# Attention values in four column tiles, and key tiles added in pairs, in a pre-norm transformer block (f32)

## The chip, the cores and the metric

The kernel runs on one core of a Trainium2 chip. The metric is the device time of one execution in microseconds (us), as the median of several runs. A core has five engines that run side by side, each with its own queue in order: TensorE (PE, products; PEld is its loading of stationary operands), VectorE (DVE), ScalarE (ACT), GpSimd (POOL) and SyncE (SP, which issues DMAs). They wait for one another through semaphores.

## The reference

A transformer block on x of shape 2 x 1024 x 1024 in float32: attention of 32 heads of width 32, then a gated feed-forward layer, both behind a layer norm and with a residual.

```python
qkv = x @ attn_qkvw + attn_qkvb                      # x: layer-normed
scores = einsum('bhqd,bhkd->bhqk', q, k) * scale     # 32 heads, 1024 queries, 1024 keys
probs = softmax(scores, axis=-1)
ctx = einsum('bhqk,bhkd->bhqd', probs, v)
x = x + ctx @ attn_ow + attn_ob
...
y = silu(xn @ W_gate.T) * (xn @ W_up.T) @ W_down.T   # 2752 wide; xn: layer-normed x
x = x + y
```

## The kernel before

The program is one long list of steps in Python, which emits instructions; what it emits first stands first in each engine's queue. `Emitter.run` (L66) merges two lists: a *fill* list of projections and feed-forward products, and a *paced* list, the attention. Each step has a planned cost (`MM4` = 855 ns for a 512-column f32 product). Attention steps that are marked as a beat are spread evenly over the planned cost of the fill; the paced steps that follow a beat are emitted at once behind it. A third kind, `em.later(delay, ...)`, is emitted when the planned clock has passed the delay.

`attention_steps` (L581) lays out the 64 heads (2 batches of 32) in beats n, eight key tiles of 128 keys to a head. One beat holds:

- `scores(kt)` (L490): two products of 512 queries into a PSUM tile `s` of 128 keys x 1024 queries; ACT copies it to `p` (L502); DVE takes the running maximum over the head's key tiles into `top` (L505, L507). With the last key tile comes `maximum()` (L511): two transposes and two reductions on DVE (L517, L518), and later a product, a reduction and two DMAs that spread the negative maximum to the tile `m`.
- `less_maximum` (L542) of the key tile 10 beats back: p + m, on DVE for key tiles 3 and 7, on POOL for the other six.
- `exponential` (L547) of the key tile 11 beats back, on ACT.
- `values` (L550) of the key tiles 12 beats back, four at a time: in the beat where key tile 3 or 7 is due, those of tiles 0 to 3 or 4 to 7 are emitted one after another.

The stationary operand of `values` is a tile `vones` of 64 columns for each key tile: the head's 32 values columns (loaded by `load_v`, L483, from DRAM on SP's queue, two beats before the head's last scores) and 32 columns of ones, written once. So one product gives 32 rows of values and 32 rows of sums. The 1024 queries are taken as two halves of 512, which go to two column tiles of TensorE (output partitions 0 to 63 and 64 to 127) and accumulate over the eight key tiles in one PSUM tile `acc`. Each f32 product leaves two records of loading and two of multiplying in the trace. `finish` (L565) copies `acc` to SBUF on ACT and stores the values and one row of the sums to DRAM, four DMA issues per head on SP's queue. There, the sums' reciprocals are made later and multiplied on by `prep_ctx` (L626).

The attention steps are cut in two lists at beat 272, that is 34 heads. The first list is paced over the projections of both batches, the second over the rest of the projections and the output projection and feed-forward layer of batch 0. During the first, POOL also builds sums of the weights (`weight_sum_steps`, L1067) for the feed-forward products (L853, L994). Batch 1's feed-forward layer runs last, without attention.

Of the kernel before, what the change touches and what calls it, by code (L numbers as in the profile page):

```python
# [24 lines left out]
class Steps:  # L25
# [6 lines left out]
    def add(self, fn, cost=0.0, needs=None, gives=None, beat=False):  # L32
        self.items.append((fn, cost, needs, gives, beat))
# [97 lines left out]
def preln_block_kernel(  # L131
# [26 lines left out]
    HPG = P // HD  # L158
    SCALE = 1.0 / math.sqrt(HD)
    MM4, MM1 = 855.0, 230.0  # L160
    QTR = 4
    LAG = 2
    RUN = 4
    RING = NT + LAG + RUN + 2

    const = ctx.enter_context(tc.tile_pool(name="const", bufs=1))
# [23 lines left out]
    def Sm(name, dt=F32):  # L190
        return ltile([P, NH], *(("S", 6) if dt == F32 else ("Sr", 3)), name, dt)
# [17 lines left out]
    def dtile(shape, name):  # L209
        return dram.tile(shape, F32, tag=name, name=name)  # L210
# [19 lines left out]
    em = Emitter()  # L230
# [212 lines left out]

    vones = [const.tile([P, NT, 2, HD], F32, tag=f"vones{i}", name=f"vones{i}") for i in range(2)]
    for t in vones:
        nc.gpsimd.memset(t[:, :, 1, :], 1.0)


    part = const.tile([P, P], F32, tag="part", name="part")
    nc.vector.memset(part, 0.0)

    class Head:
# [3 lines left out]
        def __init__(self, b, h):  # L458
            self.b, self.h, self.g = b, h, h // HPG
            self.hf = self.g // (G // NHF)  # L460
            self.name = f"{b}_{h}"
            self.v = vones[(b * HEADS + h) % 2]
            self.p = {}

        def load(self, i):

# [16 lines left out]
        def load_v(self):  # L483
            c = (self.h * HD) % NH
            nc.sync.dma_start(
                self.v[:, :, 0, :],
                dv[self.b, self.hf][:, c : c + HD].rearrange("(c p) n -> p c n", p=P),
            )

# [57 lines left out]
        def exponential(self, kt):  # L547
            nc.scalar.activation(self.p[kt], self.p[kt], AF.Exp, scale=SCALE)  # L548

        def values(self, kt):  # L550

            if kt == 0:
                self.acc = psum.tile([P, NH], F32, tag="acc", bufs=1, name=f"acc_{self.name}")
            for s in range(NS):
                nc.tensor.matmul(  # L555
                    self.acc[s * 2 * HD : (s + 1) * 2 * HD, :],
                    self.v[:, kt, :, :].rearrange("p a n -> p (a n)"),
                    self.p[kt][:, s * NH : (s + 1) * NH],
                    start=(kt == 0),
                    stop=(kt == NT - 1),  # L560
                )
            if kt == NT - 1:
                self.finish()

        def finish(self):  # L565
            part, n = divmod(self.h, HEADS // QTR)
            cs = Sm(f"cs_{self.name}")
            nc.scalar.copy(cs, self.acc)

            def store(s):  # L570
                r = 2 * s * HD
                cols = slice(s * NH, (s + 1) * NH)
                nc.sync.dma_start(
                    dctx[self.b, part][n * HD : (n + 1) * HD, cols], cs[r : r + HD, :]
                )
                nc.sync.dma_start(dsum[self.b, part][n : n + 1, cols], cs[r + HD : r + HD + 1, :])

            em.later(2500.0, lambda: store(0))
            em.later(2600.0, lambda: store(1), ("ctx", self.b, self.h))

    def attention_steps(cut):  # L581


        heads = [Head(b, h) for b in range(B) for h in range(HEADS)]
        lists = [Steps(), Steps()]
        total = len(heads) * NT
        q = lists[0]

        def load_step(k, i):
            if k < len(heads):  # L590
                q.add(lambda: heads[k].load(i), needs=("qk", heads[k].b, heads[k].g))

        for i in range(3):
            load_step(0, i)
        for n in range(total + NT + LAG + 2):
            if n == cut:
                q = lists[1]
            k, kt = divmod(n, NT)
            if n < total:
                if kt % 2 == 0 and kt < 6:  # L600
                    load_step(k + 1, kt // 2)
                if n == 0:
                    q.add(lambda: em.later(9000.0, lambda: None, ("first",)))
                    q.add(lambda: None, needs=("first",))
                if kt == NT - 2:
                    q.add(heads[k].load_v, needs=("v", heads[k].b, heads[k].hf))
                q.add(lambda k=k, kt=kt: heads[k].scores(kt), 2 * MM1, beat=True)
            else:
                q.add(lambda: None, beat=True)
            k, kt = divmod(n - NT - LAG, NT)  # L610
            if 0 <= k < len(heads):
                needs = ("max", heads[k].b, heads[k].h)
# [13 lines left out]
    def prep_ctx(b):  # L626


        def recip(i):
            cols = HEADS // QTR * S // P  # L630
            sm = small([P, cols], "sums", 1, f"sums_{b}_{i}")
            flat = lambda d: d.rearrange("h s -> (h s)").rearrange("(p c) -> p c", p=P)
            nc.sync.dma_start(sm, flat(dsum[b, i]))
            rc = small([P, cols], "recs", 1, f"recs_{b}_{i}")

            def go():
                nc.vector.reciprocal(rc, sm)
                nc.sync.dma_start(flat(drec[b, i]), rc)

            em.later(7000.0, go, ("rec", b, i))  # L640
# [487 lines left out]
    with tc.manual_schedule():  # L1128
# [80 lines left out]
            keep.items.insert(0, ffn0.items.pop())  # L1209
        tail(ffn1, 1)  # L1210

        first, second = attention_steps(HEADS * NT + 16)
# [58 lines left out]
```

## Time and profile before

| what | value |
|---|---|
| median of 3 runs | 3316.62 us (3312.51 to 3321.08) |
| the profiled execution | 3320.87 us, its span 3319.1 us |
| mean granted TensorE clock | 0.995 |
| L494, scores products | 1024 records, 467.0 us busy |
| L366, projection products | 1024 records, 469.6 us busy |
| L853, feed-forward products of 256 columns | 4704 records in two groups, 610.5 and 464.7 us busy |
| L548 on ACT, exponentials | 512 of 1060 ns |
| L502 on ACT, copies of scores | 512 of 1010 ns |
| L507 on DVE, maxima | 384 of 1222 ns |
| DMA, share of 16 engines | 41.1% and 12.2% on its two large queues |

The span runs from the first to the last instruction of the profiled execution; the rest of that execution's time lies around it. Busy time of an engine is the time in which at least one of its instructions ran: on TensorE several can run at once, so that a group's busy time is less than its count times its mean. Idle time is that of the engine just before the instruction, with the instruction or DMA that ended it.

### The profile page before, as it was taken

How to read it: one execution, taken by the hardware profiler on the slowest of the kernel's cores; microseconds unless marked ns; L12 is line 12 of the kernel's file. 1: busy time of each engine (PE TensorE's matmuls, PEld its weight loads, DVE VectorE, ACT ScalarE, POOL GpSimd, SP SyncE). 2: the span in 40 equal slices, each digit the busy share in tenths (PEclk: the TensorE clock that was granted, in tenths of full speed). 3: DMA queues.
4: the chain of work that ended last, by engine and by line, in shares of the span. 5: the costliest groups of instructions: out<-in, count | busy, mean ns of one | idle time of the engine just before them, and what ended most of it. 6: DMA issues, size and time to landing. Idle time of an engine off the chain costs nothing.

```text
span 3319.1 us, 34091 instructions
## 1 busy us (share of the span) xinstructions
PE 3246.9 (98%) x11456; PEld 1883.5 (57%) x11456; DVE 1767.1 (53%) x2454; ACT 1358.8 (41%) x1520; POOL 1187.0 (36%) x584
## 2 busy tenths in 40 slices
PE   8999998999999999999999999999999999999999
PEld 4444343444444446666664566666557777476775
DVE  3455555555555466666656675566434333344434
ACT  2465565656666455555563555555200000010000
POOL 0377666666775543333335333333210000200000
PEclk9999998999999999999999999999999999999999
DMA  4665665566555635555555455554545555645553
GB/s 166 198 210 175 204 219 183 161 211 203 191 191 168 200 108 151 154 157 153 152 164 181 127 153 158 155 154 138 166 159 153 153 153 149 196 143 152 154 153 96
DMA packets 336702, 548.64 MB, mean 165 GB/s; under 512 B 104976, under 2 KB 104976, under 8 KB 336528
## 3 DMA queue, kind: packets, MB, share of 16 engines
q1 hardware_dynamic: 281360, 414.31, 41.1%
q10 hardware_dynamic: 55168, 132.15, 12.2%
q8 instruction: 92, 1.51, 0.2%
q14 instruction: 82, 0.67, 0.1%
HBM read 454.30 MB, written 92.01 MB: 165 GB/s over the span
## 4 chain that ended last, share of the span: by engine, by line
PE 81%; DMA 6%; DVE 3%; POOL 3%; ACT 3%; issue 2%; ACTq 0%; SPq 0%; POOLq 0%; DVEq 0%
PE p L853 30%; PE pd L994 14%; PE acc L555 10%; PE pq L366 7%; PE po L711 6%; PE s L494 5%; PE pvv L422 5%; DMA m<-d 2%; POOL p L545 2%; PE pd L926 2%; DMA d<-neg 2%; ACT p L502 1%; POOL ws L1105 1%; DVE top L507 1%; PE pg L897 1%
## 5 line engine op out<-in xcount | busy, mean ns | idle before, releaser
L545 POOL TENSOR_TENSOR p<-p,m 128x1024 f32<-128x1024 f32 x384 | 928.4, 2444 | 995.3 <-DMA m<-d 717.7
L502 ACT COPY p<-s 128x1024 f32<-128x1024 f32 x512 | 516.9, 1010 | 630.7 <-PE s L494 595.9
L507 DVE TENSOR_TENSOR top<-s,top 128x1024 f32<-128x1024 f32 x384 | 469.1, 1222 | 551.1 <-ACT p L502 548.5
L548 ACT ACTIVATE p<-p 128x1024 f32<-128x1024 f32 x512 | 542.1, 1060 | 251.4 <-POOL p L545 236.8
L853 PE MATMUL p<-sum,m 128*128 128x256 f32 x2688 | 610.5, 381 | 2.7 <-DVE sum L764 1.9
L853 PEld LDWEIGHTS p<-sum,m 128*128 128x128 f32 x2688 | 508.6, 190 | 92.0 <-issue 15.2
L494 PE MATMUL s<-qs,ks 128*128 128x512 f32 x1024 | 467.0, 537 | 22.8 <-DVE top L507 22.8
L366 PE MATMUL pq<-xnT,wqk 128*128 128x512 f32 x1024 | 469.6, 596 | 0.0
L555 PE MATMUL acc<-p,vones 128*64 128x512 f32 x2048 | 468.2, 599 | 0.5 <-ACT p L548 0.4
L853 PE MATMUL p<-xn2T,m 128*128 128x256 f32 x2016 | 464.7, 380 | 0.7 <-DVE gate L876 0.7
L994 PE MATMUL pd<-wp,h 128*128 128x512 f32 x960 | 429.3, 594 | 0.2
L853 PEld LDWEIGHTS p<-xn2T,m 128*128 128x128 f32 x2016 | 380.0, 190 | 73.9 <-issue 17.0
L494 PEld LDWEIGHTS s<-qs,ks 128*128 128x128 f32 x1024 | 186.5, 191 | 233.8 <-issue 147.1
L994 PEld LDWEIGHTS pd<-wp,h 128*128 128x128 f32 x960 | 180.1, 190 | 214.3 <-issue 192.4
L366 PEld LDWEIGHTS pq<-xnT,wqk 128*128 128x128 f32 x1024 | 194.4, 191 | 187.4 <-issue 175.0
L555 PEld LDWEIGHTS acc<-p,vones 128*64 128x64 f32 x2048 | 135.3, 136 | 267.7 <-issue 211.4
L1007 DVE TENSOR_TENSOR x<-pd,x 128x512 f32<-128x512 f32 x360 | 236.8, 684 | 83.3 <-PE pd L994 83.3
L916 POOL MEMSET h<- 64x512 f32 x4 | 2.1, 524 | 678.1 <-PE pd L994 678.1
L881 ACT ACTIVATE gate<-gate 128x512 f32<-128x512 f32 x84 | 52.9, 630 | 464.5 <-DVE gate L880 464.3
L422 PE MATMUL pvv<-wv,xnT 128*128 128x512 f32 x512 | 236.8, 600 | 1.5 <-ACT xnT L267 0.9
L711 PE MATMUL po<-wo,ctx 128*128 128x512 f32 x512 | 227.6, 594 | 0.0
L545 DVE TENSOR_TENSOR p<-p,m 128x1024 f32<-128x1024 f32 x128 | 182.5, 1426 | 0.0
(90 smaller groups left out, 2049.4 us busy)
## 6 DMA issues: line engine op xcount, KB each, us to landing
m<-dws SPq DMA_DIRECT2D x336, 256.0 KB
m<-in_w_gu SPq DMA_DIRECT2D x252, 256.0 KB
wp<-ddn SPq DMA_DIRECT2D x160, 256.0 KB
qs<-dq ACTq DMA_DIRECT2D x64, 512.0 KB
ks<-dq ACTq DMA_DIRECT2D x128, 256.0 KB
m<-d SPq DMA_DIRECT2D x64, 512.0 KB
wp<-in_w_dn SPq DMA_DIRECT2D x120, 256.0 KB
raw<-in_w_gu ACTq DMA_DIRECT2D x84, 256.0 KB
```

The costliest lines, as they stand in the source:

```text
L366: nc.tensor.matmul(ps, wqk[b, g, w, hk][:, k, :], xnT[b, s][:, kc, :], start=(kc == 0), stop=(kc == KC - 1),)
L422: nc.tensor.matmul(st["ps"], xnT[b, t // TB][:, kc, (t % TB) * P : (t % TB + 1) * P], st["w"][kc], start=(kc == 0), stop=(kc == KC - 1),)
L494: nc.tensor.matmul(ps[:, s * NH : (s + 1) * NH], k[:, kt * P : (kt + 1) * P], q[:, s * NH : (s + 1) * NH], start=True, stop=True,)
L502: nc.scalar.copy(p, ps)
L507: nc.vector.tensor_tensor(self.top, ps, self.top, ALU.max)
L545: eng.tensor_tensor(p, p, self.m, ALU.add)
L548: nc.scalar.activation(self.p[kt], self.p[kt], AF.Exp, scale=SCALE)
L555: nc.tensor.matmul(self.acc[s * 2 * HD : (s + 1) * 2 * HD, :], self.v[:, kt, :, :].rearrange("p a n -> p (a n)"), self.p[kt][:, s * NH : ( ...
L711: nc.tensor.matmul(st["ps"], ctxT[b, blk][:, g, t * P : (t + 1) * P], st["w"][hf, g], start=(g == 0), stop=(g == G - 1),)
L853: nc.tensor.matmul(ps, mats[c, n][:, kc, :], rhs, start=(kc == 0), stop=(kc == hk - 1),)
L994: nc.tensor.matmul(st["pd"], lefts[n](pi)[:, j, t * P : (t + 1) * P], st["wp", pi, n, j], start=(j == 0), stop=(j == PART // 2 - 1),)
L1007: nc.vector.tensor_tensor(xs, st["pd"], xs, op)
```

## The change

Each key tile's values are computed with a stationary operand of 32 columns, the values alone (`vals`), by four products of 256 queries, one to each column tile of TensorE (output partitions 32j to 32j + 31), into the first 256 columns of `acc`. The sums come from four more products with a stationary tile of ones, into the last 256 columns.

Some key tiles are added in pairs: for a tile kt in `added`, its exponentials become p[kt] + p[kt-1]. The values of tile kt - 1 are replaced by v[kt-1] - v[kt] (`differences`, on POOL, once per head, for all its pairs), so that p[kt-1] (v[kt-1] - v[kt]) + (p[kt] + p[kt-1]) v[kt] is the same sum of values, and the ones products of tile kt - 1 are left out, since the added tile holds its exponentials. For heads 0 to 33 `added` is (1, 5), and both additions are on DVE. For heads 34 to 63 it is (1, 3, 5, 7): tiles 1 and 5 are added on POOL, tiles 3 and 7 on DVE.

The addition is emitted one beat after the tile's exponential, ahead of the values if those are due in the same beat. The planned cost of a tile's values is `MM4`, or half of it where the ones are left out. A head's results are stored by two DMA issues in place of four.

```diff
+    CUT = HEADS * NT + 16
...
-    vones = [const.tile([P, NT, 2, HD], F32, tag=f"vones{i}", name=f"vones{i}") for i in range(2)]
-    for t in vones:
-        nc.gpsimd.memset(t[:, :, 1, :], 1.0)
+    vals = [const.tile([P, NT, HD], F32, tag=f"vals{i}", name=f"vals{i}") for i in range(2)]
+    ones = const.tile([P, HD], F32, tag="ones", name="ones")
+    nc.gpsimd.memset(ones, 1.0)
+    NQ = S // HPG
...
+            self.added = (1, 5) if (b * HEADS + h) * NT < CUT else (1, 3, 5, 7)
...
+        def differences(self):
+            step = self.added[1] - self.added[0]
+            v = self.v.rearrange("p (i a) n -> p i a n", a=step)[:, :, :2, :]
+            nc.gpsimd.tensor_tensor(v[:, :, 0, :], v[:, :, 0, :], v[:, :, 1, :], ALU.subtract)
+
+        def add(self, kt):
+            if kt in self.added:
+                late = kt % RUN == RUN - 1 or len(self.added) == NT // RUN
+                eng = nc.vector if late else nc.gpsimd
+                eng.tensor_tensor(self.p[kt], self.p[kt], self.p[kt - 1], ALU.add)
+
         def values(self, kt):
             if kt == 0:
                 self.acc = psum.tile([P, NH], F32, tag="acc", bufs=1, name=f"acc_{self.name}")
-            for s in range(NS):
-                nc.tensor.matmul(
-                    self.acc[s * 2 * HD : (s + 1) * 2 * HD, :],
-                    self.v[:, kt, :, :].rearrange("p a n -> p (a n)"),
-                    self.p[kt][:, s * NH : (s + 1) * NH],
-                    start=(kt == 0),
-                    stop=(kt == NT - 1),
-                )
+            def columns(w, c, start, stop):
+                for j in range(HPG):
+                    nc.tensor.matmul(
+                        self.acc[j * HD : (j + 1) * HD, c : c + NQ],
+                        w,
+                        self.p[kt][:, j * NQ : (j + 1) * NQ],
+                        start=start,
+                        stop=stop,
+                        skip_group_check=True,
+                    )
+
+            columns(self.v[:, kt, :], 0, kt == 0, kt == NT - 1)
+            if kt + 1 not in self.added:
+                columns(ones, NQ, False, kt == NT - 1)
...
-            em.later(2500.0, lambda: store(0))
-            em.later(2600.0, lambda: store(1), ("ctx", self.b, self.h))
+            em.later(2500.0, store, ("ctx", self.b, self.h))
...
+                if kt == 0:
+                    q.add(heads[k].differences)
                 needs = ("max", heads[k].b, heads[k].h)
                 q.add(lambda k=k, kt=kt: heads[k].less_maximum(kt), needs=needs)
...
-            if 0 <= k < len(heads) and kt % RUN == RUN - 1:
-                for v in range(kt - RUN + 1, kt + 1):
-                    q.add(lambda k=k, v=v: heads[k].values(v), MM4)
+            if 0 <= k < len(heads):
+                q.add(lambda k=k, kt=kt: heads[k].add(kt))
+                if kt % RUN == RUN - 1:
+                    for v in range(kt - RUN + 1, kt + 1):
+                        cost = MM4 / 2 if v + 1 in heads[k].added else MM4
+                        q.add(lambda k=k, v=v: heads[k].values(v), cost)
```

More of the change, by code (lines that the diff above doesn't have):

```diff
@@ L461, in __init__ @@
             self.name = f"{b}_{h}"
-            self.v = vones[(b * HEADS + h) % 2]
+            self.v = vals[(b * HEADS + h) % 2]
             self.p = {}
+            self.added = (1, 5) if (b * HEADS + h) * NT < CUT else (1, 3, 5, 7)
         def load(self, i):
@@ L485, in load_v @@
             nc.sync.dma_start(
-                self.v[:, :, 0, :],
+                self.v,
                 dv[self.b, self.hf][:, c : c + HD].rearrange("(c p) n -> p c n", p=P),
@@ L568, in finish, with store @@
             nc.scalar.copy(cs, self.acc)
-            def store(s):
-                r = 2 * s * HD
-                cols = slice(s * NH, (s + 1) * NH)
+            def store():
+                ctx_ = dctx[self.b, part][n * HD : (n + 1) * HD, :]
                 nc.sync.dma_start(
-                    dctx[self.b, part][n * HD : (n + 1) * HD, cols], cs[r : r + HD, :]
-                )
-                nc.sync.dma_start(dsum[self.b, part][n : n + 1, cols], cs[r + HD : r + HD + 1, :])
-            em.later(2500.0, lambda: store(0))
-            em.later(2600.0, lambda: store(1), ("ctx", self.b, self.h))
+                    ctx_.rearrange("f (j q) -> j f q", j=HPG),
+                    cs[:, :NQ],
+                )
+                sums = dsum[self.b, part][n, :].rearrange("(j q) -> j q", j=HPG)
+                nc.sync.dma_start(sums, cs[::HD, NQ:])
+            em.later(2500.0, store, ("ctx", self.b, self.h))
     def attention_steps(cut):
@@ L1210, in preln_block_kernel @@
         tail(ffn1, 1)
-        first, second = attention_steps(HEADS * NT + 16)
+        first, second = attention_steps(CUT)
         prep0, prep1 = prep_ctx(0), prep_ctx(1)
```

## The prediction

> **What bounds the kernel now.** I read the page first (shares, chain, costliest groups), then the busy time of three stretches, then the timeline around one head's values products, then TensorE's idle gaps and the clock after them. Columns of a group: line, engine, operation, out<-in and shapes, count | busy us, mean ns of one | idle us before and who ended it.
>
> ```profile
> PE 3246.9 (98%) x11456; PEld 1883.5 (57%) x11456; DVE 1767.1 (53%) x2454; ACT 1358.8 (41%) x1520; POOL 1187.0 (36%) x584
> PE 81%; DMA 6%; DVE 3%; POOL 3%; ACT 3%; issue 2%; ACTq 0%; SPq 0%; POOLq 0%; DVEq 0%
> L545 POOL TENSOR_TENSOR p<-p,m 128x1024 f32<-128x1024 f32 x384 | 928.4, 2444 | 995.3 <-DMA m<-d 717.7
> L555 PE MATMUL acc<-p,vones 128*64 128x512 f32 x2048 | 468.2, 599 | 0.5 <-ACT p L548 0.4
> L545 DVE TENSOR_TENSOR p<-p,m 128x1024 f32<-128x1024 f32 x128 | 182.5, 1426 | 0.0
> ```
>
> TensorE is busy 98% of the span and is 81% of the chain; the products that the change touches wait 0.5 us in all. So TensorE sets the time: a product saved is time saved, and a new wait in its queue is time lost in full.
>
> ```profile
> 1144.00:1770.00 626.00, 617.72 (x2375) 382.68 (x2375) 397.27 (x543) 338.64 (x362) 243.66 (x109) 1.00 0.52 156
> 139.00:1144.00 1005.00, 960.02 (x3013) 421.35 (x3011) 555.63 (x595) 601.29 (x655) 667.37 (x333) 0.99 0.60 192
> ```
>
> Stretches (length, then busy PE, PEld, DVE, ACT, POOL, clock, DMA share, GB/s). Heads 0 to 33 run in 139 to 1144 us, heads 34 to 63 until 2379 us. In the second stretch TensorE idles 8 us of 626, so nothing there can absorb a wait.
>
> The timeline where head 41's first four key tiles are multiplied (start, us, engine, line):
>
> ```profile
> 1435.72 1.03 PE L494 MATMUL s<-qs,ks 128*128 128x512 f32 x2
> 1436.67 3.65 PE L555 MATMUL acc<-p,vones 128*64 128x512 f32 x16
> 1436.84 1.01 ACT L502 COPY p<-s 128x1024 f32<-128x1024 f32 x1 [3.65 <-PE s L494]
> 1437.88 1.23 DVE L507 TENSOR_TENSOR top<-s,top 128x1024 f32<-128x1024 f32 x1 [0.20 <-ACT p L502]
> 1439.21 0.71 DVE L517 STREAM_TRANSPOSE m<-top 128x512 f32<-128x512 f32 x1
> 1439.96 0.69 DVE L518 TENSOR_REDUCE part<-m 128x16 f32<-128x512 f32 x1
> 1440.56 0.70 DVE L517 STREAM_TRANSPOSE m<-top 128x512 f32<-128x512 f32 x1
> 1441.30 0.69 DVE L518 TENSOR_REDUCE part<-m 128x16 f32<-128x512 f32 x1
> ```
>
> A scores product (L494) is followed at once by the values products (L555): 16 records in 3.65 us, two abreast, a pair every 0.43 us (the weight loads of such a group start at 1438.01, 1438.44, 1438.87). While TensorE multiplies, the same scores go through ACT's copy, DVE's maximum and, for a head's last key tile, four more DVE instructions, until 1441.99, 5.3 us after the group began.
>
> **Part 1, products saved.** Two records of 512 columns take 0.43 us side by side. Now a key tile's values are 8 records of 256 columns in four tiles: four abreast they also take 0.43 us, and its ones another 0.43. Before, a head took 16 x 0.43 = 6.88 us. A tile whose successor is added needs no ones: heads 0 to 33 have 8 + 6 = 14 groups of 8 (6.02 us), the rest 8 + 4 = 12 (5.16 us). Saved: 34 x 0.86 + 30 x 1.72 = 29 + 52 = 81 us. The trace shows two abreast, never four. Bounds per group: 0.43 (four) and 0.86 (the two abreast of L555). I take 0.43: the pair's records start 7 ns apart and each runs as fast as a lone one, and neither waits for the other's second pass, so tiles look independent.
>
> The Trainium skill speaks against it: TensorE: Matmul & The Clock Gate, section Back-to-back issue gap, gives about 81 ns for each load-and-multiply pair in a stream of 128-column products. No run here has so dense a stream. By that page's figure a group of 8 would take an estimated 0.65 us and the whole change would come to about 3,695 us.
>
> **Part 2, the new wait (heads 34 to 63).** Key tiles 3 and 7 are added on DVE, and the add stands in DVE's queue directly behind the maximum of the scores product that precedes the values group on TensorE (for tile 3, behind the four head-maximum instructions too). Values of tile 3 wait for the add. In the rows above: maxima done at 1441.99, add 1.43 us (L545 on DVE, same shapes), landing 0.05 later: 1443.47. TensorE gets through tiles 0 to 2 (1 + 2 + 1 groups, 1.72 us) at 1438.39. Stall 5.1 us. Read so for each head from 34 to 62, the stall is 5.1 us in the median and 152 us in all; for tile 7, where only copy and maximum stand before the add, 2.2 us in the median and 77 us over 28 heads. (Head 62's second half and head 63 have no scores ahead of them: no stall.) Behind the waiting product stand the next scores and all of the feed-forward products; they go late by the full stall, since the stretch has no idle time to give back. Sum 229 us; bounds 57 less each 1.72 (131, if groups take 0.86) and 229.
>
> Heads 0 to 33 add tiles 1 and 5, two beats ahead of the values: their exponential ends 4.9 us (median) before the group, so an add of 1.43 fits. Cover gone, each would cost up to 1.43.
>
> **Part 3, the clock after a stall.** TensorE's idle gaps of this trace (in brackets) and the clock behind them:
>
> ```profile
> 544.75 1.11 PE L259 MATMUL pt_a<-ident,x 128*128 128x128 f32 x4 [5.21 <-DVE lo L381]
> 1771.58 2.93 PE L926 MATMUL pd<-wd,h 128*128 128x512 f32 x3 [4.44 <-DVE x L1007]
> 575.17 0.73 PE L494 MATMUL s<-qs,ks 128*128 128x512 f32 x2 [1.86 <-DVE top L507]
> ...
> 541.90:548.80 6.90, 4.05 (x9) 2.57 (x10) 5.31 (x6) 6.06 (x8) 6.90 (x5) 0.51 0.45 142
> 576.10:579.50 3.40, 3.40 (x5) 1.33 (x4) 3.37 (x5) 1.96 (x2) 3.40 (x3) 0.50 0.07 13
> 1770.70:1777.60 6.90, 6.02 (x7) 2.53 (x8) 6.90 (x7) 1.06 (x1) 5.19 (x2) 0.51 0.00 0
> ```
>
> All three gaps over 4.4 us led to 6.8 us at half clock, with 4.0 to 6.0 us of products in it: 2.7 us lost each on average. Of six gaps from 1.8 to 2.6 us three led to 3.4 us at half clock, 1.7 lost. So 29 x 2.7 + 28 x 0.85 = 102 us. Bounds: 0 (the 3.5 us gap at 386 us had no drop) and 29 x 3.0 + 28 x 1.7 = 135.
>
> The same page of the Trainium skill, Part 1, lets the clock fall after an idle window of about 3.4 us; by that the 2.2 us stalls are free and the long ones cost an estimated 1.7 us, 49 in all. The 1.86 us gap above contradicts it, so the rows count.
>
> **Part 4, the rest.** DVE gets 34 x 2 x 1.43 = 97 us in the first stretch, where it is 55% busy; 97 is the bound if none is hidden, 0 if all. TensorE now waits there some 73 us for L507; with 97/556 more DVE work I take 17% of that, 13 us. POOL gets 30 x 2 adds of 2.44 us (row L545 on POOL) and 64 small differences; POOL is 39% busy in the second stretch and idles 26 us per head waiting for m, and v has landed at least 11 us before the first L545 of each head, so 0; uncovered, 2.44 each, 146 us. The exponentials before POOL's adds of tiles 1 and 5 end 13 us (median) ahead of the values, so these are not waited for: 0. Stores go from four DMA issues per head to two on SP: 0. The planner counts the products at the new, lower cost; its delays only grow in real time: 0.
>
> **Sum.** 3320.9 (profiled execution) - 81 + 13 + 229 + 102 = 3584; the median of the runs lies 4 us under that execution: **3580 us**.
>
> **Rivals.** (a) The clock stays up: 3580 - 102 = 3478. For: one 3.5 us gap without a drop; against: three of three longer ones. (b) Fewer than four abreast. At 0.86 per group: 34 x 5.16 + 30 x 3.44 = +278 in place of -81, stalls 131, clock about 25 (gaps of 3.4 us), 13: 3321 + 447 - 4 = 3764. For: four abreast is nowhere in the trace, and 16 instructions per 0.43 us is four times what L555 needs now. Against: the independent pairs. (c) Faster: the add is done when TensorE comes to tile 3 (7), because DVE takes it before the maximum. Then 3317 - 81 + 13 = 3249. It decides as soon as the stalls and their clock cost less than 68 us in all, some 1.2 us each. Against: the queue order above, and copy plus maximum plus add alone are 3.7 us against 1.72. (d) The change does not take place: the built program has 4,640 more matmul records and 128 more DVE instructions; no weight.
>
> **How the numbers follow.** Forecast 0.55, its own range 3530 to 3620 (clock 50 to 135); (a) or a partial drop 0.16; (b) and between 0.24; (c) 0.04, and 0.01 for a result within 0.3%, which is what measurement can tell from no change. The range leaves out the lowest of (a), (c) and the end of (b): 3465 to 3730. Faster 0.04, same 0.01, slower 0.95.
>
> **What would show it.** Right: L575 groups with TensorE idle some 5 and 2 us before tile 3 and 7, released by the DVE add, from 1144 us on only; half clock in that stretch; heads 0 to 33 in slightly less time than 1005 us. Wrong: no idle time at L575 from DVE, or the first stretch growing (then four abreast fails).

## The result, and the profile after

The changed kernel takes 3742.43 us (median of 4 runs, 3726.51 to 3747.26), the kernel before 3317.97 us: a ratio of 1.127 [1.124, 1.131]. The profiled execution has a span of 3742.5 us at a mean granted clock (the share of its full speed that TensorE was granted) of 0.947; before, 3319.1 us at 0.995.

From the page of the changed kernel: busy time by engine, the clock in 40 slices, the shares of the chain, and three of the costliest groups (columns as in the prediction):

```profile
PE 3332.1 (89%) x16096; PEld 2007.1 (54%) x16096; DVE 2028.9 (54%) x2582; ACT 1360.5 (36%) x1520; POOL 1417.8 (38%) x707
PEclk9999999999999999888888989989999999999999
PE 48%; DVE 10%; ACT 2%; issue 2%; DMA 1%; POOL 0%; SPq 0%; ACTq 0%; DVEq 0%; POOLq 0%
L498 PE MATMUL s<-qs,ks 128*128 128x512 f32 x1024 | 476.8, 547 | 46.1 <-DVE top L511 46.1
L575 PE MATMUL acc<-p,vals 128*32 128x256 f32 x4096 | 327.4, 412 | 289.4 <-DVE p L565 289.4
L575 PE MATMUL acc<-p,ones 128*32 128x256 f32 x2592 | 229.1, 429 | 0.0
```

The values products, which waited 0.5 us in the kernel before, now wait 289 us for the addition (L565) on DVE; the scores products (L498) wait 46 us for DVE's maximum. The clock digits show the loss where heads 34 and on run.

Windows of the changed kernel, cut at head 0's first values group, head 34's, and the last one's end (length, busy PE, PEld, DVE, ACT, POOL, clock, DMA share, GB/s):

```profile
138.90:1226.40 1087.50, 967.26 (x5736) 474.12 (x5735) 670.05 (x664) 600.83 (x655) 712.11 (x368) 0.96 0.57 177
1226.40:2797.50 1571.10, 1299.12 (x6621) 829.48 (x6620) 919.88 (x1124) 659.23 (x702) 651.17 (x293) 0.90 0.40 120
2797.50:3742.50 945.00, 936.93 (x3397) 639.52 (x3394) 387.90 (x712) 57.92 (x111) 39.07 (x32) 1.00 0.49 152
```

The same cuts of the kernel before have lengths of 1005.4, 1235.0 and 939.5 us. A stretch is TensorE's idle time, plus half of the time that it was busy while its clock was granted at 0.5 ("lost" to half clock), plus the rest, which is its work at full clock:

| us | first: before, after | second: before, after |
|---|---|---|
| TensorE idle | 45.0, 120.2 | 11.8, 272.0 |
| lost to half clock | 8.4, 38.2 | 4.7, 124.1 |
| work at full clock | 952.0, 929.1 | 1218.5, 1175.0 |
| length | 1005.4, 1087.5 (+82) | 1235.0, 1571.1 (+336) |

The change does save work on TensorE: 23 + 43 = 66 us. It pays for it with 336 us of idle time and 149 us of clock. What ended the idle time, from the waits of TensorE in the changed kernel (us in total, times, longest), first stretch and then second:

```profile
PE acc L575 <- DVE p L565: 49.5, 26, 4.5
PE s L498 <- DVE top L511: 46.1, 24, 5.2
```

```profile
PE acc L575 <- DVE p L565: 239.9, 58, 11.8
PE pd L1024 <- DVE x L1037: 15.9, 9, 4.3
```

The timeline of the changed kernel around head 42's first half shows one such wait, and the windows behind it the clock:

```profile
1659.44 0.82 PE L498 MATMUL s<-qs,ks 128*128 128x512 f32 x2
1660.20 1.07 PE L575 MATMUL acc<-p,vals 128*32 128x256 f32 x16
1660.30 1.01 ACT L506 COPY p<-s 128x1024 f32<-128x1024 f32 x1 [1.35 <-PE s L498]
1661.09 0.61 PE L575 MATMUL acc<-p,ones 128*32 128x256 f32 x8
1661.35 1.23 DVE L511 TENSOR_TENSOR top<-s,top 128x1024 f32<-128x1024 f32 x1 [2.39 <-ACT p L506]
1661.52 0.61 PE L575 MATMUL acc<-p,vals 128*32 128x256 f32 x8
...
1664.77 0.69 DVE L522 TENSOR_REDUCE part<-m 128x16 f32<-128x512 f32 x1
1665.37 1.22 DVE L565 TENSOR_TENSOR p<-p,p 128x1024 f32<-128x1024 f32 x1
1666.64 1.08 PE L575 MATMUL acc<-p,vals 128*32 128x256 f32 x8 [4.51 <-DVE p L565]
1667.49 1.08 PE L575 MATMUL acc<-p,ones 128*32 128x256 f32 x8
```

```profile
1666.40:1669.70 3.30, 3.06 (x19) 1.61 (x20) 0.18 (x1) 0.00 (x0) 0.00 (x0) 0.50 0.00 0
1670.00:1673.30 3.30, 3.30 (x18) 2.84 (x17) 0.94 (x3) 1.21 (x2) 0.00 (x0) 1.00 0.44 120
```

TensorE finishes the groups of tiles 0 to 2 at 1662.13 and stands for 4.51 us, because the addition of tile 3 stands on DVE behind the maximum of the scores that TensorE had just made. At full clock groups of 8 follow one another every 0.43 us (1661.09, 1661.52): four abreast. After the wait they need 0.85 us (1666.64, 1667.49), as the clock is at 0.50 until 1669.8.

DVE's large operations in the second stretch, first in the kernel before and then in the changed one:

```profile
L507 DVE TENSOR_TENSOR top<-s,top 128x1024 f32<-128x1024 f32 x170 | 207.6, 1221 | 206.4 <-ACT p L502 206.4
L545 DVE TENSOR_TENSOR p<-p,m 128x1024 f32<-128x1024 f32 x60 | 80.7, 1345 | 0.0
```

```profile
L511 DVE TENSOR_TENSOR top<-s,top 128x1024 f32<-128x1024 f32 x170 | 207.7, 1222 | 194.7 <-ACT p L506 194.3
L549 DVE TENSOR_TENSOR p<-p,m 128x1024 f32<-128x1024 f32 x60 | 114.3, 1905 | 0.0
L565 DVE TENSOR_TENSOR p<-p,p 128x1024 f32<-128x1024 f32 x60 | 97.1, 1618 | 0.0
```

The maximum, which reads one operand from PSUM (where TensorE's products land), takes what it took. The operations on two tiles in SBUF (the memory of all other tiles here) are dear: less-maximum went from 1345 to 1905 ns, and an addition takes 1618 where the timeline shows 1.22 us for one beside an idle POOL.

### The profile page after: what moved, and what is told of

Read it like the earlier page. It is cut to its first block, busy times and chain, and to the rows that moved or that the text cites. A ratio compares the mean times of both kernels' runs of the same rounds, so it can differ in the third digit from the quotient of the medians.

```text
span 3742.5 us, 43317 instructions
## 1 busy us (share of the span) xinstructions
PE 3332.1 (89%) x16096; PEld 2007.1 (54%) x16096; DVE 2028.9 (54%) x2582; ACT 1360.5 (36%) x1520; POOL 1417.8 (38%) x707
## 4 chain that ended last, share of the span: by engine, by line
PE 48%; DVE 10%; ACT 2%; issue 2%; DMA 1%; POOL 0%; SPq 0%; ACTq 0%; DVEq 0%; POOLq 0%
PE p L883 26%; PE pd L1024 11%; PE po L741 4%; PE acc L575 2%; DVE p L565 2%; PE s L498 2%; ACT p L506 2%; DVE top L511 2%; PE pd L956 1%; DVE p L549 1%; DVE m L521 1%; DVE part L522 1%; DVE x L1037 1%; PE pg L927 1%; DMA ctx<-dctx 0%
## 5 line engine op out<-in xcount | busy, mean ns | idle before, releaser
L549 POOL TENSOR_TENSOR p<-p,m 128x1024 f32<-128x1024 f32 x384 | 975.6, 2562 | 509.2 <-DMA m<-d 488.1
L511 DVE TENSOR_TENSOR top<-s,top 128x1024 f32<-128x1024 f32 x384 | 468.3, 1220 | 514.4 <-ACT p L506 511.3
L883 PE MATMUL p<-sum,m 128*128 128x256 f32 x2688 | 636.4, 391 | 7.3 <-DVE gate L910 3.9
L575 PE MATMUL acc<-p,vals 128*32 128x256 f32 x4096 | 327.4, 412 | 289.4 <-DVE p L565 289.4
L883 PEld LDWEIGHTS p<-sum,m 128*128 128x128 f32 x2688 | 524.5, 197 | 102.7 <-issue 14.7
L498 PE MATMUL s<-qs,ks 128*128 128x512 f32 x1024 | 476.8, 547 | 46.1 <-DVE top L511 46.1
L883 PE MATMUL p<-xn2T,m 128*128 128x256 f32 x2016 | 480.7, 390 | 5.1 <-DVE up L908 4.5
L1024 PE MATMUL pd<-wp,h 128*128 128x512 f32 x960 | 459.0, 627 | 16.1 <-DVE x L1037 14.2
L883 PEld LDWEIGHTS p<-xn2T,m 128*128 128x128 f32 x2016 | 391.8, 196 | 80.5 <-issue 18.0
L565 POOL TENSOR_TENSOR p<-p,p 128x1024 f32<-128x1024 f32 x60 | 142.3, 2371 | 697.3 <-ACT p L552 680.6
L575 PEld LDWEIGHTS acc<-p,vals 128*32 128x32 f32 x4096 | 115.5, 114 | 433.7 <-DVE p L565 330.5
L498 PEld LDWEIGHTS s<-qs,ks 128*128 128x128 f32 x1024 | 190.9, 195 | 250.1 <-issue 142.2
L1024 PEld LDWEIGHTS pd<-wp,h 128*128 128x128 f32 x960 | 189.6, 201 | 244.4 <-issue 209.0
L575 PE MATMUL acc<-p,ones 128*32 128x256 f32 x2592 | 229.1, 429 | 0.0
```

The costliest lines, as they stand in the source:

```text
L498: nc.tensor.matmul(ps[:, s * NH : (s + 1) * NH], k[:, kt * P : (kt + 1) * P], q[:, s * NH : (s + 1) * NH], start=True, stop=True,)
L511: nc.vector.tensor_tensor(self.top, ps, self.top, ALU.max)
L549: eng.tensor_tensor(p, p, self.m, ALU.add)
L575: nc.tensor.matmul(self.acc[j * HD : (j + 1) * HD, c : c + NQ], w, self.p[kt][:, j * NQ : (j + 1) * NQ], start=start, stop=stop, skip_grou ...
L883: nc.tensor.matmul(ps, mats[c, n][:, kc, :], rhs, start=(kc == 0), stop=(kc == hk - 1),)
L1024: nc.tensor.matmul(st["pd"], lefts[n](pi)[:, j, t * P : (t + 1) * P], st["wp", pi, n, j], start=(j == 0), stop=(j == PART // 2 - 1),)
```

## The experiments

All edits are against the changed kernel; a ratio is to the kernel before, run on the same chip, and "first" and "second" are the lengths of the two stretches. Where `added` is empty for some heads, the line `if kt == 0:` ahead of `differences` also becomes `if kt == 0 and heads[k].added:`.

**Which part costs what: no additions, the first stretch's alone, the second's alone.**

```diff
-            self.added = (1, 5) if (b * HEADS + h) * NT < CUT else (1, 3, 5, 7)
+            self.added = ()                                                              # e1_no_adds
+            self.added = (1, 5) if (b * HEADS + h) * NT < CUT else ()                    # e2_first_only
+            self.added = () if (b * HEADS + h) * NT < CUT else (1, 3, 5, 7)              # e3_second_only
```

> Four column tiles and separate ones, but no key tiles added (no additions, no differences; every tile has its ones). Theory A (the loss is the wait for the additions and the clock behind it; four tiles run abreast): 16 groups of 8 records at 0.43 us per head, as much as before, so 3300 to 3335 us, and no idle time of TensorE within the values groups. Rival B (the finer products themselves disturb the stream, and a part of the 424 us is theirs): over 3350.

> Additions only in heads 0 to 33 (tiles 1 and 5, on DVE). In the changed kernel the stretch of these heads grew from 1005 to 1088 us in place of shrinking by 29. Theory A (DVE comes too late to the addition of tile 1 there, because it shares a beat with the less-maximum and the maximum and both are stretched while POOL works): the stretch stays at 1075 to 1100 us and the whole comes to 3390 to 3420. Rival B (that stretch grew for another reason, such as what the later heads' additions do): 3290 to 3320, the products saved being won.

> Additions only in heads 34 to 63 (tiles 1, 3, 5, 7). Theory A (the two stretches are independent): first stretch as before, 1000 to 1015 us; second as in the changed kernel, 1571; total 3640 to 3670, with some 240 us of idle time before the values of tiles 3 and 7. Rival B (the first stretch's lateness is carried into the second): total under 3600.

| | median us | ratio | first | second |
|---|---|---|---|---|
| e1_no_adds | 3325.73 | 1.0017 [1.0005, 1.0028] | 1006.5 | 1235.6 |
| e2_first_only | 3403.28 | 1.0255 [1.0234, 1.0276] | 1085.7 | 1236.0 |
| e3_second_only | 3661.48 | 1.1027 [1.1004, 1.1049] | 999.6 | 1577.1 |

Column tiles alone cost next to nothing (6.8 us): no wait of note in front of the values, both stretches as before. That settles the four tiles: two groups of 8 in four tiles take the time of a key tile's two half-array products. Each set of additions keeps its cost without the other: 84 us for the first stretch and 343 for the second, over the 3318.9 of the kernel before, and their sum is the whole.

**The addition one beat earlier**, right behind the exponential, with the products of the changed kernel.

```diff
                 q.add(lambda k=k, kt=kt: heads[k].exponential(kt))
+                q.add(lambda k=k, kt=kt: heads[k].add(kt))
...
-                q.add(lambda k=k, kt=kt: heads[k].add(kt))
                 if kt % RUN == RUN - 1:
```

> All additions, each emitted one beat earlier, right behind its exponential, so that on DVE it stands ahead of the maximum of the scores that directly precede the values. Theory A (the place in DVE's queue makes the wait): idle time within the values groups falls from 289 us to under 60, half clock to under 100 us, total 3250 to 3340. Rival B (DVE is too slow for the additions wherever they stand, since POOL stretches them to 2.5 us): the idle time stays over 150 us and the total over 3500.

3408.54 us, 1.0272 [1.0248, 1.0296]; first 1065.8, second 1260.0. The waits in front of the values go from 289 to about 14 us, so it was the place in DVE's queue. But the total met neither window. Two of its waits (us in total, times, longest):

```profile
DVE p L565 <- ACT p L552: 50.0, 44, 3.2
PE s L498 <- DVE top L511: 67.3, 35, 4.9
```

The addition now stands in DVE's queue ahead of its own input: it waits for the exponential, the maximum waits behind it, and the scores products wait for the maximum. In the two stretches TensorE now idles 168 us, against 57 before; these waits (22.8 us before) are the largest item, the feed-forward products' waits for DVE (21 us) the next. Another 48 us are lost to half clock, 13 before. The saved products pay a part of that, and 90 us are left over the kernel before.

**The same beat, but ahead of the scores**, so that the next maximum stands behind the addition. For the second stretch on DVE and POOL, for the second with all four on DVE, and for the first:

```diff
+        def ahead(n):
+            k, kt = divmod(n - NT - LAG - 2, NT)
+            if 0 <= k < len(heads):
+                heads[k].add(kt)
...
-                q.add(lambda k=k, kt=kt: heads[k].scores(kt), 2 * MM1, beat=True)
+                q.add(lambda k=k, kt=kt, n=n: (ahead(n), heads[k].scores(kt)), 2 * MM1, beat=True)
...
-                q.add(lambda k=k, kt=kt: heads[k].add(kt))
...
+                late = True                    # e6_second_ahead_dve alone
```

> Additions only in heads 34 to 63, and each emitted just ahead of the scores of the beat in which the values may be due, so that it stands ahead of that beat's maximum in DVE's queue, and a beat of fill products behind its exponential. Theory A (place in the queue, and an addition that waits for its exponential holds DVE up): idle time within the values groups under 25 us, second stretch 1190 to 1235 us, total 3275 to 3315. Rival B (DVE has no room for the additions beside POOL, wherever they stand): second stretch over 1250, total over 3335.

> As the run before, with tiles 1 and 5 added on DVE too, none on POOL. In the changed kernel DVE's additions of two SBUF operands took 1.21 us alone and 2.2 to 2.5 us while POOL worked. Theory C (the residue comes from DVE and POOL holding each other up): DVE's less-maximum falls back from 1.9 us to about 1.35 and the total is 5 to 20 us under the run before. Rival (the residue comes from the sum of DVE's work): the total is 5 to 30 us over it.

> Additions only in heads 0 to 33, on DVE, each emitted just ahead of the beat's scores. Theory A (DVE's beat overflows, so the wait moves but stays): values wait under 10 us in place of 48, scores wait for the maximum over 45 us; stretch 1040 to 1085, total 3360 to 3400. Rival (the place alone decides, as for tiles 3 and 7 later): stretch under 1010, total under 3320.

| | median us | ratio | stretch of the edit | values wait | scores wait for the maximum |
|---|---|---|---|---|---|
| e5_second_ahead | 3394.58 | 1.0215 [1.02, 1.023] | 1303.3 | 65 | - |
| e6_second_ahead_dve | 3387.83 | 1.0191 [1.0172, 1.0209] | 1299.5 | 77 | - |
| e8_first_ahead | 3380.72 | 1.017 [1.0155, 1.0185] | 1058.3 | 6.5 | 70 |

In the second stretch most of the stall is gone (240 us of waits in the changed kernel), but 65 us stay: the queue order was not the whole cause. The timeline of e5_second_ahead shows one part of what is left:

```profile
2223.11 7.46 POOL L549 TENSOR_TENSOR p<-p,m 128x1024 f32<-128x1024 f32 x3 [7.49 <-DMA m<-d]
2225.49 2.88 DVE L997 TENSOR_TENSOR s<-h 128x512 f32<-128x512 f32 x1
2228.90 2.75 DVE L565 TENSOR_TENSOR p<-p,p 128x1024 f32<-128x1024 f32 x1
2231.71 0.64 PE L575 MATMUL acc<-p,vals 128*32 128x256 f32 x8 [4.26 <-DVE p L565]
```

POOL works without a break on two-input operations; two of DVE's take 2.88 and 2.75 us meanwhile, and the values wait 4.26 us. Of the 65 us, 36 end with an addition that took over 1.3 us; in the other 30 it took its 1.22 us and came late because of what stood ahead of it. With no additions on POOL (e6_second_ahead_dve) DVE's less-maximum falls back to 1298 ns, but DVE has twice the additions, and the total is 7 us less, with intervals of the ratios that still overlap. In the first stretch the wait moves: from the values (6.5 us left) to the scores (70).

**The first stretch's additions on POOL.**

```diff
             self.added = (1, 5) if (b * HEADS + h) * NT < CUT else ()
...
-                late = kt % RUN == RUN - 1 or len(self.added) == NT // RUN
+                late = False
```

> Additions only in heads 0 to 33, with both on POOL in place of DVE. Theory A (in this stretch DVE's beat overflows: maximum, less-maximum and addition in one beat): scores wait for DVE's maximum some 20 us as before (50 with the additions on DVE), values for the addition under 20; stretch 980 to 1020 us, total 3285 to 3325. Rival B (POOL, 66% busy before, overflows instead, and holds DVE up): stretch over 1045, total over 3355.

3390.74 us, 1.0204 [1.0187, 1.0221]; first 1074.2. The values wait for POOL (36 us), the scores for the maximum (55), and 64 of DVE's 68 less-maximum operations now run beside POOL for more than half of their time (35 in the kernel before); the mean of all is 1743 ns. POOL is busy 80% of the stretch, DVE 53%: moving the addition to POOL moves the waits, and what POOL does holds DVE up.

**Is it the length of the addition?** In the first stretch, DVE does a one-input multiplication by 1 in its place.

```diff
-                eng.tensor_tensor(self.p[kt], self.p[kt], self.p[kt - 1], ALU.add)
+                eng.tensor_scalar(self.p[kt], self.p[kt], 1.0, None, ALU.mult)
```

> As the run with additions in heads 0 to 33 alone, but in the place of each addition DVE multiplies the tile by 1.0: one SBUF operand, so the sums of the pairs are not formed. Theory C (it is the length of the additions, stretched by POOL): the operation takes 0.6 to 1.0 us, also beside POOL, and the first stretch falls from 1086 us to 985 to 1035. Rival (any work of DVE at that place does it, since the values then wait for DVE's queue): the stretch stays over 1060.

3390.77 us, 1.0203 [1.0185, 1.022]; first 1073.6, against 1085.7 with the addition. The operations on this line of e13_first_one_input (shortest, median and longest in ns, first and last start in us):

```profile
L565 DVE TENSOR_SCALAR p<-p x68: 673/804/2866, 136.0 to 1185.0; 128x1024 f32<-128x1024 f32 x68
```

The 29 of these operations during which POOL does nothing take 0.67 to 0.69 us, a good two fifths less than such an addition (1.21), and yet four fifths of the loss stay (67 us of 84, each against the kernel before of its own comparison): beside POOL it too takes up to 2.87 us, and it still stands in the queue between two maxima. So the length of an undisturbed addition isn't what decides. Since the shorter operation is stretched as well, the run doesn't separate the stretching from the place in the queue.

**Fewer additions, or all on POOL, in the second stretch.** The first uses tiles 1 and 5 alone in their place; the others are a beat earlier (the edit of e4_early).

```diff
-                late = kt % RUN == RUN - 1 or len(self.added) == NT // RUN
+                late = False
...
+            self.added = () if (b * HEADS + h) * NT < CUT else (1, 5)          # e9_second_pool2, e11_second_pool2_early
+            self.added = () if (b * HEADS + h) * NT < CUT else (1, 3, 5, 7)    # e10_second_pool4
+            self.added = () if b * HEADS + h < 37 else (1, 3, 5, 7)            # e12_pool4_from37
```

> Additions only in heads 34 to 63, only of tiles 1 and 5, both on POOL at the place the change gives them (two beats ahead of the values). DVE gets no addition. Theory C (the residue in the runs with well placed additions is DVE's operations on two SBUF operands, stretched while POOL works, in a queue that TensorE waits for): no waits of the values, second stretch 1205 to 1228 us against 1235, total 3288 to 3315, 2 to 30 us under before. Rival (POOL's additions alone hold DVE up enough to eat the 26 us of products saved): second stretch 1235 or more, total 3320 or more.

> Additions only in heads 34 to 63, of tiles 1, 3, 5 and 7, all on POOL, each emitted one beat earlier, right behind its exponential. Theory C: the exponential of tile 3 ends 3 us (median) ahead of the values, the addition takes 2.4, so that few values wait (under 30 us in all); second stretch 1190 to 1235, total 3275 to 3325. Rival (POOL comes too late for tiles 3 and 7, since its queue also holds the less-maximum, and holds DVE up more): values wait over 60 us for POOL, total over 3335.

> As the run with tiles 1 and 5 added on POOL in heads 34 to 63, but each addition one beat earlier, right behind its exponential. There, 31 of 59 less-maximum operations of DVE ran while POOL worked (1.90 us in the mean), against 8 of 59 in the run with all four additions early on POOL (1.40). Theory C (that coincidence makes the 20 us of waits for DVE): if the earlier place takes POOL's addition away from DVE's less-maximum, the mean falls to about 1.4, the stretch to 1205 to 1225 us and the total to 3290 to 3312; if the mean stays at 1.9, the stretch stays over 1240 and the total over 3325. Rival (the number of POOL's additions decides, not their time): total within 10 us of that run, whatever the mean.

> The run with all four additions early on POOL, but from head 37 on, since 11 of its 30 us of waits for POOL fell in heads 34 to 36, where the paces change. Expected: 27 x 1.72 = 46 us of products saved at the most, waits for POOL some 18 us, total 3300 to 3318, so faster than the kernel before by up to 0.5%. Rival (the waits come with any first heads of the pairs): total 3318 or more.

| | median us | ratio | second |
|---|---|---|---|
| e9_second_pool2 | 3340.09 | 1.0063 [1.0049, 1.0077] | 1255.9 |
| e11_second_pool2_early | 3342.51 | 1.0063 [1.0047, 1.0079] | 1257.2 |
| e10_second_pool4 | 3317.57 | 0.9998 [0.999, 1.0007] | 1232.0 |
| e12_pool4_from37 | 3319.38 | 0.9997 [0.9987, 1.0008] | 1227.6 |

Less-maximum on DVE in the second stretch, in e9_second_pool2 and then in e10_second_pool4:

```profile
L549 DVE TENSOR_TENSOR p<-p,m 128x1024 f32<-128x1024 f32 x59 | 114.1, 1934 | 0.0
```

```profile
L549 DVE TENSOR_TENSOR p<-p,m 128x1024 f32<-128x1024 f32 x59 | 82.4, 1396 | 0.0
```

With two additions on POOL the values don't wait (1 us), but some 31 of these 59 run beside POOL for more than half of their time, against 8 with four additions, and the feed-forward products (L1024) wait 20 us for DVE, against 3. So the run with more additions is the faster one, which suggests that what matters is whether DVE's two-input operations meet POOL's. In e9_second_pool2 27 of them meet POOL's own less-maximum and only 3 an addition: the additions shift POOL's other work. Every run with exactly the additions of tiles 1 and 5 on POOL in this stretch has 31 to 33 such meetings, every other run 4 to 13. Moving the two additions a beat earlier (e11_second_pool2_early) left the 31 where they were; why four fall apart from DVE's work and two do not is open. The four on POOL give the products' saving back as waits for POOL (30 us) and others; leaving them out for heads 34 to 36 (e12_pool4_from37) brought POOL's to 11 us and the total no lower. These two are the best versions that compute everything, and they equal the kernel before.

**What the saved products are worth.** The additions are left out but the products stay saved (e14_sums_left_out); the differences too (e15_products_alone); or differences alone, with every ones product kept (e16_differences_alone).

```diff
-                eng.tensor_tensor(self.p[kt], self.p[kt], self.p[kt - 1], ALU.add)
+                pass                              # e14_sums_left_out, e15_products_alone
...
-                if kt == 0:
-                    q.add(heads[k].differences)   # e15_products_alone
...
-            if kt + 1 not in self.added:
+            if True:                              # e16_differences_alone
...
-                q.add(lambda k=k, kt=kt: heads[k].add(kt))         # e16_differences_alone
...
-                        cost = MM4 / 2 if v + 1 in heads[k].added else MM4
+                        cost = MM4                # e16_differences_alone
```

> The changed kernel with the additions of exponentials left out (the products are those of the change, the differences of values too; the sums of the pairs are not formed). Theory A (all of the loss is due to the additions): no waits within the values groups, first stretch 970 to 990 us, second 1183 to 1195, total 3230 to 3260. Rival B (a part of the products' 81 us is not there to be won, or is lost elsewhere): total 3265 or more.

> Neither the additions nor the differences of values, so neither the sums of the pairs nor the replaced values are formed; the products are those of the change. Theory D (POOL's differences, waiting for the values' DMA, hold up POOL's queue): first stretch 970 to 985 us, scores wait some 20 us for the maximum, total 3260 to 3285. Theory E (the first stretch is paced by ACT, POOL and DVE, not by TensorE, so that products saved there turn into waits): first stretch 1000 to 1030 us, total 3295 to 3312.

> The differences of values, but no additions and all the ones products at their full planned cost: TensorE does what it does in the run without additions (first stretch 1006.5 us), and the values are the replaced ones without the sums of the pairs. Theory D: first stretch 1020 us or more, total 3335 or more. Theory E: within 6 us of that run, 3320 to 3332 in all.

| | median us | ratio | first | second |
|---|---|---|---|---|
| e14_sums_left_out | 3307.55 | 0.9947 [0.9929, 0.9965] | 1025.0 | 1200.6 |
| e15_products_alone | 3308.18 | 0.9962 [0.9949, 0.9975] | 1030.0 | 1196.0 |
| e16_differences_alone | 3331.52 | 1.0027 [1.0012, 1.0042] | 1010.0 | 1236.8 |

With the additions left out, and the differences too, the saved products are worth 0.4 to 0.5%, not the 81 us (2.4%) of the forecast. The second stretch gets 40 us shorter than with all ones products (e1_no_adds, 1235.6); the first gets 24 us longer. Windows and waits of the first stretch, in e1_no_adds:

```profile
139.50:1146.00 1006.50, 964.19 (x6277) 485.16 (x6277) 556.97 (x595) 603.08 (x656) 667.47 (x333) 0.99 0.60 192
```

```profile
POOL p L549 <- DMA m<-d: 251.3, 29, 13.1
ACT p L552 <- POOL p L549: 212.5, 96, 7.4
PE s L498 <- DVE top L511: 19.9, 14, 2.7
```

and in e15_products_alone, where DVE, ACT and POOL do the same work:

```profile
139.50:1169.50 1030.00, 948.33 (x5735) 468.17 (x5734) 556.55 (x596) 600.43 (x656) 664.49 (x333) 0.98 0.60 187
```

```profile
POOL p L549 <- DMA m<-d: 291.7, 33, 13.8
ACT p L552 <- POOL p L549: 275.6, 110, 9.7
PE s L498 <- DVE top L511: 55.1, 29, 5.4
```

TensorE has 542 records less, and DVE, ACT and POOL the same work as in e1_no_adds. POOL waits longer for the maximum (`m`), the exponentials for POOL and the scores for DVE; TensorE's idle time rises from 42.3 to 81.7 us and what the half clock costs from 12.1 to 18.8. That is clear of the noise: in the runs that keep every ones product and add nothing in this stretch, it takes 999.6 to 1010.0 us. So the saving isn't won there, though TensorE is 96% busy. What sets the pace instead is argued and not shown: ACT, DVE and POOL are each busy under 67% of the stretch, and POOL itself stands waiting for the maximum's DMA, so it would be the chain from scores over maximum and exponentials back to TensorE, and not one engine's load. There is a rival: the planned cost of a tile without ones is halved, as in the change, so the planner also sets the beats closer together in its list, and the order of the steps changes with the products. No run saves the products and keeps the planned cost. Differences alone cost little (e16_differences_alone is within 6 us of e1_no_adds, in another comparison).

## Why the prediction was right and wrong

The direction held, and in the second stretch the mechanism; in the first stretch the mechanism failed. The forecast of 3580 us was 162 us short: by the profiled executions 98 us in the first stretch, 57 in the second and 5 in the last.

- **Four abreast** held: in the trace four records of a group start 7 ns apart, and the next four 216 ns later, 0.43 us for 8. The measured total is close to the 3764 of rival (b), but not by its mechanism: groups of 8 take 0.43 us and no more at full clock. Nor does the prediction's sign "the first stretch growing (then four abreast fails)" read rightly: that stretch grew, and four abreast did not fail. The figure of the Trainium skill that was set against it (TensorE: Matmul & The Clock Gate, Back-to-back issue gap, about 81 ns) does not hold for these products in four column tiles: 0.432 us / 8 = 54 ns per load-and-multiply pair.
- **The wait of heads 34 to 63** held: 240 us in 58 waits against 229 forecast. Tile 3: 150 us, 4.5 in the median (152 and 5.1 forecast); tile 7: 90 us, 2.9 in the median (77 and 2.2). That the order in DVE's queue causes most of it is shown by e5_second_ahead. That the sum came within 5% is in part luck: the forecast priced every addition at 1.43 us, while 33 of the 58 that were waited for took 1.22 and the other 25 took 1.54 to 3.33, beside POOL; the mean of all of DVE's additions is 1.77. The forecast also took the queue order for the whole cause: 65 us stay in e5_second_ahead without it. Some 20 us of other idle time came along, the feed-forward products' wait for DVE the most of it.
- **The clock** held in kind, rival (a) is out: 119 us more lost in the second stretch, against 102. The first stretch lost another 30, where none was forecast.
- **The step that failed** is the sentence "So TensorE sets the time: a product saved is time saved", applied to heads 0 to 33. It is true of the second stretch (e15_products_alone: 40 us shorter, of 52 forecast), and wrong in the first, where 29 us were credited and the same run is 24 us longer. The profile before gave a hint: 45 us of idle time, half of it scores that wait for the maximum, in a stretch where the forecast gave the saving in full and 13 us for DVE. Against these 13 us stand 75 us more of idle time and 30 of clock. The "some 73 us" from which the 13 was worked out were misread, too: 22.8 us are TensorE's wait for L507, and the other 50 the same waits in the row of its weight loading (PEld), which is no further idle time of TensorE.
- **"so an add of 1.43 fits"** failed with it. The exponential was early enough, as forecast, but the forecast did not ask what else DVE does in those beats. The first stretch of the changed kernel:

```profile
733.11 2.36 POOL L549 TENSOR_TENSOR p<-p,m 128x1024 f32<-128x1024 f32 x1
734.50 1.22 DVE L511 TENSOR_TENSOR top<-s,top 128x1024 f32<-128x1024 f32 x1 [0.15 <-ACT p L506]
735.65 2.15 DVE L549 TENSOR_TENSOR p<-p,m 128x1024 f32<-128x1024 f32 x1
736.66 8.97 POOL L549 TENSOR_TENSOR p<-p,m 128x1024 f32<-128x1024 f32 x3
736.72 0.64 PE L575 MATMUL acc<-p,vals 128*32 128x256 f32 x8
737.72 3.36 DVE L565 TENSOR_TENSOR p<-p,p 128x1024 f32<-128x1024 f32 x1
741.00 2.54 DVE L511 TENSOR_TENSOR top<-s,top 128x1024 f32<-128x1024 f32 x2
741.13 0.92 PE L575 MATMUL acc<-p,vals 128*32 128x256 f32 x8 [3.78 <-DVE p L565]
```

Maximum, less-maximum and addition stand one behind the other; the last two take 2.15 and 3.36 us beside POOL. The values of tile 1 wait 3.78 us, and the next two maxima, whose copies ended at 737.5 and 739.8, start at 741.00: 26 such waits of the values, 49.5 us, and 46.1 us of scores that wait for the maximum. The additions, with the differences, add 56 us to the 24 of the products (1085.7 in e2_first_only against 1030.0). e13_first_one_input shows that an operation that is shorter when undisturbed would still have cost most of it in this place.

The Trainium skill has a page that bears on this, and it would have warned: SBUF — State Buffer, section SBUF: two separate sides, says that VectorE and GpSimd share a port pair as an exclusive lock, held for a whole instruction, when VectorE has two SBUF inputs and GpSimd reads SBUF. The runs agree: the 59 of DVE's additions in the changed kernel during which POOL does nothing take 1.20 to 1.22 us, the others up to 3.39; POOL's own operations take 2.99 us each in the row at 736.66 (8.97 for 3) against 2.36 for the one at 733.11; and the maxima, with one operand in PSUM, stay at 1.22. The one-input operation that also took 2.87 us can be held to the same page only by its other case, a two-port mode of VectorE, which no run here tests.

Three things stay open: what sets the pace of the first stretch, why two additions on POOL meet DVE's less-maximum and four do not, and some 15 us of the saved work (66 us measured as work at full clock, 81 forecast). A version that keeps the saving in the second stretch alone and hides every addition could win an estimated 40 us, what e15_products_alone shows there, or 35 with the differences (e14_sums_left_out); none of the versions tried that form the sums came below the kernel before. Multiplying the values a beat later wasn't tried.

## What to carry to other kernels

Before a saved product is credited as time, read the bottleneck's idle time in that very stretch and who ended it: where it already waits for other engines, less work on it may win nothing, as in heads 0 to 33 here, and each new wait can cost clock as well. Before an operation is put in a queue, ask what stands in front of it there: here an operation that TensorE waited for stood behind one that needed TensorE's latest product, and the change's second half came to 0 us in place of 343 once its additions were on POOL and a beat earlier. And an operation on two SBUF operands on DVE is priced by what POOL does at that moment (1.22 us alone here, up to 3.39 beside it), not by its mean.

## What the runs showed of the hardware

- Column tiles of 32 run four abreast in f32 at no loss (e1_no_adds: 1235.6 us for the second stretch, 1235.0 before): starts 7 ns apart, each tile again after 216 ns, its two passes included.
- How long TensorE must idle for the clock to fall, in the changed kernel's trace: of 23 gaps from 1.0 to 1.8 us none was followed by half clock, of 28 from 1.8 to 2.6 us 17, of 13 from 2.6 to 3.4 us 10, of 51 longer ones all. It mostly lasts 3.41 or 6.83 us (44 and 30 of 79 times; up to 13.65), beginning 2 to 5 us after TensorE fell idle. The Trainium skill's idle window of about 3.4 us (TensorE: Matmul & The Clock Gate, Part 1) is here the length from which the drop is sure, not the one from which it occurs.
- DVE beside POOL: operations with two SBUF operands of 128x1024 f32 take up to 3.39 us instead of 1.22, a one-input one up to 2.87 instead of 0.67 (e13_first_one_input); with one operand in PSUM they are not slowed (1220 ns in the mean of 384, at most 1226).
